# A two-layer graph network on one core: fewer and larger transfers, segment marks picked by matrix products, and a looser tie of gathers to VectorE

## The chip, the cores and the metric

The kernel runs on one core of a Trainium2 chip. The metric is the device time of one execution in microseconds (us). A run gives the time of the whole execution. The profile is of one execution of its own: its span runs from the first to the last recorded instruction, and its execution is a little longer than the span. The engines are PE (TensorE), DVE (VectorE), ACT (ScalarE), POOL (GpSimd) and SP (SyncE, which here only issues transfers). PEld is the weight load that comes before each matmul.

## The reference: what is computed

There are 6250 nodes with 256 features each and 106250 edges, sorted by target; 6250 of the edges lead from a node to itself.

```python
# layer 0: a message per edge, by relation r (0 or 1), summed by target
msgs = where(rel == r, relu(relu(x[src] @ W[r].T + b[r]) @ W[r].T + b[r]), msgs)
agg = segment_sum(msgs, dst)
i, f, g, o = split(agg @ W_ih.T + b_ih + b_hh, 4)
hn = sigmoid(o) * tanh(sigmoid(i) * tanh(g))
x = layernorm(x + mlp3(hn))
# layer 1: attention over the edges and one more self loop per node, 4 heads of 64
h = x @ W
e = leaky_relu(a_src[src] + a_dst[dst], 0.2)
alpha = exp(e - segment_max(e, dst)[dst]) / segment_sum(...)
y = layernorm(segment_sum(h[src] * alpha, dst) + bias + x) * gamma + beta
out = layernorm(x + relu(y))
```

The two expensive things are the reads of a row per edge (x[src] through a table of messages, then h[src]) and the sums by target.

## The kernel before

**Preparation (0 to some 190 us).** The self edges are taken out of the list; 782 tiles of 128 edges are left (`TC`). Seven tiles make a window (`WT`), two windows a group, so there are 112 windows (`NW`) and 56 groups (`NG`). A window's targets lie within 64 slots (`SLOTS`) of nodes; for each edge the kernel stores its slot number in DRAM (`slots`, in bf16, eight tiles to a window). It also stores the marks (`cuts`): for each edge 0 where it has the same target as the edge before it, and a very large negative number where a new target begins. At the same time PE computes both messages of every node into a DRAM table (`parts0`).

**Layer 0 (to some 1175 us).** For every tile GpSimd issues one indirect transfer (`gather`, L1720 in the profile) that fetches 128 rows of 256 numbers by index. The tile is multiplied by a one-hot matrix of slots (L2162), which sums it by target. When a group is done, `turn` and `update` run the gates and the small network for four groups at a time (`quads`; at the end for two groups and then for one). `update` keeps three rows of 256 numbers per node in `keep3`: the layer's output, the output plus the bias, and h. They are stored in DRAM (`kept`, L2107), one group at a time. The rows that layer 1 gathers go to `rows1` (L2097).

**Layer 1 (to the end).** GpSimd gathers a row of 260 numbers per edge (h and the logit) into `G`, a ring of ten windows (70 tiles). The first 21 gathers (`EARLY`) are issued before the last rows of layer 0 are there, and `complete` adds what they lack. Groups are taken in pairs, the last four one by one (`pairs`), 26 pairs and 4 singles in all. For each:

- `ahead` loads the slot numbers (`dB`, L2301, one transfer per window, the window's numbers repeated over 64 partitions) and the marks (`cut`, L2308, one transfer per group, one row per tile and head). It compares the slot numbers with the partition's number (L2315, `ohT`), multiplies by what is known of the targets (L2319) and sums three parts (L2336, `of`).
- `weights` turns the logits (L2359), finds the maximum of each segment by four scans over `cut` (L2366 to L2377), and takes the exponential into `exs` (L2390).
- `weighted` makes a one-hot matrix per group (L1826) and multiplies the gathered rows by their weights (L2405, L2410, L2411, `gw`), a window at a time.
- `sum1` multiplies one or two tiles a step by the one-hot matrix (L2526). At the first tile of a group it loads that group's kept rows (`k3`, L2516).
- `finish` divides, adds the kept rows, normalises twice (L2443 to L2472) and stores the result (L2477). The last group's result is shifted by a product (L2482) and stored at L2491.

**What sets the order.** The schedule is written out by hand: each engine executes its instructions in the order in which the program issues them. The program runs in steps; in layer 1, step t issues the gather of tile t and handles tile t - 4. The parts above are Python generators (chains), and `yield n` lets n steps pass. One generator, `aheads`, goes through all pairs in order: a pair begins at step 14 times its first group (a single group 14 steps earlier than that), or when the pair before it has ended. Buffers come from `ring`, which hands out n tiles of one name in turn. `Pace` ties the gathers to VectorE: at the end of each step it notes VectorE's last instruction, and `hold` lets a gather wait for the note of a given number of steps before it. In layer 1 that distance is 8 steps (`AHEAD1`) and more at the beginning.

```python
move = gather(G[w][:, t - WT * w, :], rows1, idx1[:, t : t + 1])
pace.hold(move, t, AHEAD1 + max(0, 6 * WT - (t - EARLY) // 4))
```

The distance is thus 50 at tile 21 and falls by one in four tiles until it is 8, at tile 189. SyncE issues all the loads and stores named here except the gathers, in the order of the program, so a store that waits for its data holds the loads behind it.

Of the kernel before, what the change touches and what calls it, by code (L numbers as in the profile page):

```python
# [42 lines left out]
P = 128  # L43
N = 6250
D = 256
# [37 lines left out]
BLOCK1, BLOCK2 = 33, 40  # L83
AHEAD_G = range(AHEAD_W // 2)
LATE = 3
AHEAD0 = 2 * WT
AHEAD1 = WT + 1
NOROW = NP + SLOTS - 1
# [656 lines left out]
def gnn_kernel(  # L745
# [47 lines left out]
    slots = dram.tile([NW, (WT + 1) * P], BF16, name="slots")  # L793
    cuts = dram.tile([(NC + 1) * CT, P], F32, name="cuts")
    srcs = dram.tile([EARLY, P], F32, name="srcs")
    kept = dram.tile([NG, P, 3 * D], F32, name="kept")
    packed = dram.tile([2 * BLOCKS, HB], I32, name="packed")

    const = ctx.enter_context(tc.tile_pool(name="fconst", bufs=1))
# [844 lines left out]
def fast(  # L1644
# [57 lines left out]
    def windows_of(g):  # L1702
        return range(2 * g, 2 * g + 2)
# [137 lines left out]
    with (  # L1841
# [134 lines left out]
        def update(groups, aT):  # L1976
# [62 lines left out]
            mv = ring(up, [P, 4, 2], F32, "fmv", 3)  # L2039
            rstd = ring(up, [P, 4], F32, "frstd", 3)  # L2040

            keep3 = [ring(up, [P, 3, D], F32, "keep3", 6) for g in groups]
            for i, g in enumerate(groups):
                u = everyone
                p3 = ring(upp, [P, 4 * P], F32, "fpg", 5)[:, : 2 * P]
# [34 lines left out]
            for i, g in enumerate(groups):  # L2080
                u = everyone
                ph = ring(upp, [P, 4 * P], F32, "fpg", 5)[:, : D + 2 * H]
                for k in range(2):
                    nc.tensor.matmul(  # L2084
                        ph[u, :], hs[i][:, k, u], Wx[:, k, :], start=(k == 0), stop=(k == 1)
                    )
                hr = ring(up, [P, D + 2 * H], F32, "hr", 3)
                if g >= NG - LATE:
                    hr = rows_l[:, g - (NG - LATE), :]
                nc.scalar.copy(hr[u, :], ph[u, :])  # L2090
                nc.scalar.copy(keep3[i][u, 2, :], ph[u, :D])

                in_order(stored, g)
                for w in windows_of(g):
                    if w in at_w:
                        to = rows1[bass.ds(at_w[w], SLOTS), :]
                        keep_row(g, nc.sync.dma_start(to, hr[half_of(w), :HA]))  # L2097
                if g == NG - 1:
                    move = nc.gpsimd.indirect_dma_start(
                        out=rows1,  # L2100
                        out_offset=bass.IndirectOffsetOnAxis(ap=tail_i, axis=0),
                        in_=hr[:, :HA],
                        in_offset=None,
                    )
                    keep_row(g, move)
                yield 1
                nc.sync.dma_start(kept[g, u, :], keep3[i][u, :, :].rearrange("p c f -> p (c f)"))  # L2107

                nd = ring(up, [P, 2, H], F32, "nd", 3)
                left = ring(up, [P, 2, H], F32, "left", 3)  # L2110
                nd3 = ring(up, [P, 3, 2, H], BF16, "nd3", 3)
                nc.vector.tensor_copy(nd[u, 0, :], hr[u, HA : HA + H])  # L2112
                nc.vector.tensor_copy(nd[u, 1, :], hr[u, D:HA])
                lg = loop[u, g, :]
                nc.vector.tensor_add(lg, nd[u, 0, :], nd[u, 1, :])
                n3 = [nd3[u, c, :, :] for c in range(3)]
                nc.vector.tensor_copy(n3[0], nd[u, :, :])
                nc.vector.scalar_tensor_tensor(lg, lg, 0.2, lg, op0=OP.mult, op1=OP.max)
                nc.vector.tensor_sub(left[u, :, :], nd[u, :, :], n3[0])
                nc.vector.tensor_copy(n3[1], left[u, :, :])  # L2120
                nc.vector.tensor_sub(n3[2], left[u, :, :], n3[1])
                yield slow
                for s, w in enumerate(windows_of(g)):
                    nc.scalar.copy(
                        node3[half_of(w), g, s, :, :],
                        nd3[half_of(w), :, :, :].rearrange("p c a h -> p c (a h)"),
                    )

        got, ohs, sums, turned, stored, loop0, rows_x = {}, {}, {}, {}, [], {}, {}
        run.start(weights_of_logits())  # L2130

        def order_of(g):
# [113 lines left out]
    with (  # L2246
# [45 lines left out]
        def ahead(pair, box):  # L2292

            cut = ring(ep, [P, P + 1], F32, "cut", 3)
            of = ring(ep, [P, 2 * GS, 2 * H], F32, "of", 3)
            box.update(cut=cut, of=of)
            dBs = []
            for g in pair:
                dB = ring(ep, [P, W8, P], BF16, "dB", 3)
                for w in windows_of(g):  # L2300
                    nc.sync.dma_start(  # L2301
                        dB[half_of(w), :, :].rearrange("p j e -> p (j e)"),
                        at(slots, w * W8 * P, [[0, SLOTS], [1, W8 * P]]),
                    )
                dBs.append(dB)
            for i, g in enumerate(pair):
                n = len(tiles_in(g)[1])
                nc.sync.dma_start(  # L2308
                    cut[i * GS * H : (i * GS + n) * H, :],
                    at(cuts, tiles_in(g)[0][0] * P, [[P, n], [0, H], [1, P + 1]]),  # L2310
                )
            yield 8
            for i, (g, dB) in enumerate(zip(pair, dBs)):
                ohT = ring(ep, [P, W8, P], BF16, "ohT", 2)
                nc.vector.tensor_scalar(ohT, dB, slot_p, None, op0=OP.is_equal)  # L2315
# [26 lines left out]
                yield 1  # L2342

        def weights(pair, box):
# [10 lines left out]
                return ap.rearrange("p (t h) -> p t h", h=H)  # L2355

            yield 1
            pe = ring(tps, [P, P], F32, "turn", 2)
# [10 lines left out]
            pd = ring(tps, [P, P], F32, "turn", 2)  # L2369
# [11 lines left out]
            pm = ring(tps, [P, P], F32, "turn", 2)  # L2381
# [36 lines left out]
        def finish(g, ps):  # L2418
# [1 line left out]
            u = everyone  # L2420
            n = u.stop
            at_w = lows_of(ws)
            k3 = k3s[g]
# [74 lines left out]
        def sum1():  # L2498
# [12 lines left out]
            if g not in sums:  # L2511
                sums[g] = ring(eps, [P, D + 2 * H], F32, "fps1", 2)
                left[g] = len(tiles_in(g)[1])
                u = everyone
                k3s[g] = ring(fp, [P, 3, D], F32, "k3", 3)
                nc.sync.dma_start(k3s[g][u, :, :].rearrange("p c f -> p (c f)"), kept[g, u, :])  # L2516
            begins = left[g] == len(tiles_in(g)[1])
            left[g] -= 1
            j = t - 2 * WT * g
# [20 lines left out]
        for q in range(2):  # L2540
            nc.vector.tensor_scalar(
                shift[:, q, :], iota_f, own_q[:, q : q + 1], None, op0=OP.is_equal
            )
        run.start(aheads())
        pace = Pace(0)
        t = 0
        while t < TC + LAG or late or queue or run.chains:
            if EARLY <= t < TC:
                w = t // WT
                if t % WT == 0:  # L2550
                    G[w] = ring(rowsp, [P, WT * HA], F32, "G", 10).rearrange(
                        "p (j f) -> p j f", f=HA
                    )
                move = gather(G[w][:, t - WT * w, :], rows1, idx1[:, t : t + 1])
                pace.hold(move, t, AHEAD1 + max(0, 6 * WT - (t - EARLY) // 4))
            k = t - LAG
            if 0 <= k < TC:
                if k < EARLY:
# [91 lines left out]
```

## Time and profile before

| what | us |
|---|---|
| median of 10 runs | 2185.58 |
| lowest and highest run | 2180.65, 2188.49 |
| the profiled execution | 2182.08 |
| its span | 2180.3 |
| PE busy | 1556.4 |
| GpSimd (POOL) busy | 1529.5 |
| VectorE (DVE) busy | 1285.4 |
| ScalarE (ACT) busy | 509.9 |
| first gather of layer 0 starts | 153.7 |
| first ordinary gather of layer 1 starts | 1176.6 |
| last gather starts | 2133.8 |

The page of the profile gives the span in 40 slices of 54.5 us, each digit the busy share of an engine in tenths. A group of instructions is a line, an engine, an operation and its tiles ("G<-rows,fidx" reads `rows` and `fidx` and writes `G`), with its count, its busy time in us, the mean duration of one in ns, and the time for which the engine stood idle just before them, with what ended most of it. "issue" is an idle time for which the profile shows no other reason. In a timeline the columns are the start and the duration in us, the engine, the line, the operation, and in brackets the idle time before. SyncE's transfers are in the trace with the time that SyncE took to issue them: 0.60 us for `dB`, 0.90 us for `cut`, 0.52 us for the store of `kept` and 0.44 us for its load (medians). The gathers of layer 1 bring 128 rows of 1040 bytes each.

### The profile page before, as it was taken

To read this page: it belongs to the slowest core of one execution; us is meant where nothing else is said; L and a number is where in the kernel's file an instruction comes from. 1 tells how busy PE (TensorE), PEld (TensorE's weight loads), DVE (VectorE), ACT (ScalarE), POOL (GpSimd) and SP (SyncE) were. 2 spreads that over 40 slices of the span, in tenths; PEclk is the share of its full clock that TensorE was granted. 3 is DMA by queue.
4 is the path that set the end of the run, shared out by engine and by line. 5 is a ranking of instruction groups with operands and counts; after the bars stand their busy time and mean duration, and the time that the engine had idled before them with its cause. 6 is when DMAs were issued, how large, how long until landed. Compare 5 with 4: busy or idle time off the path is not lost. (4 is left out here: it accounts for less than half of the span.)

```text
span 2180.3 us, 23466 instructions
## 1 busy us (share of the span) xinstructions
PE 1556.4 (71%) x5945; PEld 795.5 (36%) x5945; DVE 1285.4 (59%) x3508; ACT 509.9 (23%) x1571; POOL 1529.5 (70%) x1610
## 2 busy tenths in 40 slices
PE   8996898888888988888996565455554545454564
PEld 5654443333333333333454333232322223232332
DVE  8773244333333334333544788877787777787786
ACT  3332022222212221222343121212111121211212
POOL 2317777777777777777776777777777777777771
PEclk9998899998999989998998776676767666676777
DMA  5337546555545554555556455655556565555551
GB/s 163 127 104 211 170 137 173 144 171 167 153 145 156 172 164 139 147 172 165 171 166 184 126 158 147 165 157 147 156 145 160 146 165 144 159 153 151 158 152 48
DMA packets 164627, 334.53 MB, mean 153 GB/s; under 512 B 42658, under 2 KB 75157, under 8 KB 164482
## 3 DMA queue, kind: packets, MB, share of 16 engines
q0 software_dynamic: 76048, 207.99, 35.6%
q1 hardware_dynamic: 86257, 121.90, 18.0%
q10 hardware_dynamic: 2176, 3.05, 0.5%
q8 instruction: 49, 0.80, 0.2%
q14 instruction: 97, 0.79, 0.1%
HBM read 280.25 MB, written 52.53 MB: 153 GB/s over the span
## 5 line engine op out<-in xcount | busy, mean ns | idle before, releaser
L1720 POOL DMA_INDIRECT G<-rows,fidx x761 | 726.6, 955 | 231.8 <-issue 123.7
L1720 POOL DMA_INDIRECT G<-parts,fidx x722 | 690.6, 956 | 221.6 <-issue 160.1
L2526 PE MATMUL fps<-gw,oh 128*64 128x264 f32 (+1 forms) x1674 | 438.1, 469 | 244.4 <-DVE gw L2411 244.3
L2162 PE MATMUL fps<-G,oh 128*64 128x257 f32 (+1 forms) x1674 | 495.6, 423 | 125.7 <-DMA G<-parts,fidx 101.7
L2526 PEld LDWEIGHTS fps<-gw,oh 128*64 128x64 f32 (+1 forms) x1674 | 224.7, 166 | 412.5 <-DVE gw L2411 263.1
L2162 PEld LDWEIGHTS fps<-G,oh 128*64 128x64 f32 (+1 forms) x1674 | 195.1, 148 | 401.4 <-issue 183.9
L2411 DVE TENSOR_TENSOR gw<-G,bank 128x1792 f32<-128x1792 f32 (+1 forms) x167 | 248.9, 1490 | 62.3 <-ACT gw L2410 58.8
L2001 PE MATMUL fpg<-faT,fWihT 128*128 128x512 f32 (+2 forms) x432 | 170.2, 517 | 0.2 <-DVE faT L1937 0.2
L1919 DVE TENSOR_SCALAR kind<-fps 128x1 f32<-128x1 f32 x112 | 12.4, 152 | 230.7 <-PE fps L2162 230.7
L1826 DVE TENSOR_TENSOR oh<-bank,fslot 128x1024 f32<-128x1024 f32 x106 | 128.8, 1215 | 10.0 <-ACT bank L2390 7.2
L2359 PE MATMUL turn<-fident,e 128*120 128x128 f32 (+2 forms) x30 | 12.4, 415 | 151.5 <-ACT e L2571 151.5
L1609 POOL DMA_INDIRECT G<-parts,fidx x60 | 56.9, 948 | 67.3 <-DMA parts<-fms 49.4
L1575 PE MATMUL fpm<-fWrT,fhT 128*128 128x256 f32 x392 | 94.3, 393 | 8.0 <-DVE fms L1583 6.3
L2001 PEld LDWEIGHTS fpg<-faT,fWihT 128*128 128x128 f32 x432 | 70.6, 189 | 67.4 <-issue 56.8
L2112 DVE COPY nd<-hr 128x4 f32<-128x4 f32 x53 | 10.1, 190 | 142.9 <-ACT hr L2090 142.9
L1561 PE MATMUL fph<-fxc,fWrT 128*128 128x512 f32 (+1 forms) x208 | 90.0, 582 | 5.3 <-DMA frel_i<-in_rel_dram 4.7
L2460 ACT ACTIVATE frs<-fmv,eps_c 128x1 f32<-128x1 f32 x112 | 32.9, 294 | 237.5 <-DVE gw L2405 154.0
L2466 ACT ACTIVATE fy<-fy,frs 128x256 f32<-128x256 f32 x112 | 66.8, 597 | 87.3 <-DVE frs L2463 46.2
L1575 PEld LDWEIGHTS fpm<-fWrT,fhT 128*128 128x128 f32 x392 | 75.3, 196 | 27.7 <-issue 8.9
L2084 PE MATMUL fpg<-Wx,fyT 128*128 128x264 f32 x224 | 76.1, 469 | 3.0 <-ACT fyT L2075 3.0
L2579 ACT COPY e<-G 128x28 f32<-128x28 f32 x112 | 23.8, 213 | 180.1 <-DMA G<-rows,fidx 143.3
L2359 PEld LDWEIGHTS turn<-fident,e 128*120 128x120 f32 (+2 forms) x30 | 4.7, 157 | 165.3 <-ACT e L2571 164.0
(347 smaller groups left out, 1965.6 us busy)
## 6 DMA issues: line engine op xcount, KB each, us to landing
kept<-keep SPq DMA_DIRECT2D x56, 384.0 KB
k<-kept SPq DMA_DIRECT2D x56, 384.0 KB
dB<-slots SPq DMA_DIRECT2D x112, 128.0 KB
loop<-parts SPq DMA_DIRECT2D x110, 128.0 KB
parts<-fms SPq DMA_DIRECT2D x49, 256.0 KB
G<-parts,fidx POOLq DMA_INDIRECT x782
G<-rows,fidx POOLq DMA_INDIRECT x761
fxn<-in_x_dram SPq DMA_DIRECT2D x110, 64.0 KB
```

The lines of the kernel that those rows point to most:

```text
L1561: nc.tensor.matmul(ph[:, :cols], WrT_s[:, r, k, m * P : (m + 1) * P], xc[:, k, :cols], start=(k == 0), stop=(k == 1),)
L1575: made = nc.tensor.matmul(pm[:, r, :], hT[:, r, k, j * P : (j + 1) * P], WrT_s[:, r, k, :], start=(k == 0), stop=(k == 1),)
L1609: nc.gpsimd.indirect_dma_start(out=of[:, n % WT, :D], out_offset=None, in_=parts0[: 2 * P * block, :], in_offset=bass.IndirectOffsetOnAxis ...
L1720: return nc.gpsimd.indirect_dma_start(out=to_tile, out_offset=None, in_=table, in_offset=bass.IndirectOffsetOnAxis(ap=idx, axis=0),)
L1826: nc.vector.tensor_tensor(to[:, :nj, :], iota_s[:, None, :].to_broadcast([P, nj, SLOTS]), of[:, :, None].to_broadcast([P, nj, SLOTS]), op= ...
L2001: nc.tensor.matmul(pg[:, :cols], WihT_s[:, k, c * P : (c + 1) * P], aT[:, k, :cols], start=(k == 0), stop=(k == 1),)
L2084: nc.tensor.matmul(ph[u, :], hs[i][:, k, u], Wx[:, k, :], start=(k == 0), stop=(k == 1))
L2162: nc.tensor.matmul(sums[g][to, :], ohj, got[t], start=begins, stop=ends)
L2411: nc.vector.tensor_mul(gw[:, :, :D].rearrange("p j (h f) -> p j h f", h=H), of[:, :n, :D].rearrange("p j (h f) -> p j h f", h=H), ex[:, o ...
L2460: nc.scalar.activation(r, mv[u, k, 1:2], AF.Ln, bias=eps_c[u])
L2466: nc.scalar.activation(y, y, AF.Identity, bias=m, scale=r)
L2526: nc.tensor.matmul(sums[g][to, :], ohj, gw, start=begins, stop=ends)
```

## The change

There are four edits.

1. **Kept rows.** `kept` is stored and loaded for two groups at once: `keep3` is a ring of three tiles for two groups instead of six for one, `k3` a ring of two tiles for two groups instead of three for one. The store is issued after the second group, the load at the first tile of the first group. The last four groups are still stored and loaded one by one.
2. **Slot numbers.** One transfer brings both windows of a group.
3. **Marks.** The first two pairs load them as before. For all others, the whole list of marks lies in SBUF (`cut_all`, one transfer, started at step 21): seven blocks of 113 rows of 129 numbers. A matmul with a matrix of zeros and ones (`pick`) copies the row of each tile to its four heads in PSUM, and ScalarE copies that to `cut`. The PSUM tiles named "turn", of which there are two, become 129 columns wide and serve this too. The pause in `ahead` after the loads is 12 steps for pairs instead of 8.
4. **Tie.** The distance between gather and VectorE falls by one in six tiles instead of four, so it reaches 8 at tile 273.

```diff
-            keep3 = [ring(up, [P, 3, D], F32, "keep3", 6) for g in groups]
+            for g in groups:
+                if g % 2 == 0:
+                    kept_of[g // 2] = ring(up, [P, 2, 3, D], F32, "keep3", 3)
+            keep3 = [kept_of[g // 2][:, g % 2, :, :] for g in groups]
...
-                nc.sync.dma_start(kept[g, u, :], keep3[i][u, :, :].rearrange("p c f -> p (c f)"))
+                if len(groups) == 1:
+                    nc.sync.dma_start(
+                        kept[g // 2, :, g % 2, :], keep3[i].rearrange("p c f -> p (c f)")
+                    )
+                elif g % 2:
+                    nc.sync.dma_start(
+                        kept[g // 2], kept_of[g // 2].rearrange("p i c f -> p i (c f)")
+                    )
...
-                dB = ring(ep, [P, W8, P], BF16, "dB", 3)
-                for w in windows_of(g):
+                dB = ring(ep, [P, W8 * P], BF16, "dB", 3)
+                nc.sync.dma_start(
+                    dB, at(slots, 2 * g * W8 * P, [[W8 * P, 2], [0, SLOTS], [1, W8 * P]])
+                )
+                dBs.append(dB)
+            if pair in pairs[:2]:
+                for i, g in enumerate(pair):
...
+            else:
+                o = pair[0] % 2 * GS * H
+                n = ((len(pair) - 1) * GS + len(tiles_in(pair[-1])[1])) * H
+                pc = ring(tps, [P, P + 1], F32, "turn", 2)
+                nc.tensor.matmul(
+                    pc[:n, :],
+                    pick[:, pair[0] % 8 // 2, o : o + n],
+                    cut_all[:, pair[0] // 8, :],
+                    start=True,
+                    stop=True,
+                )
+                nc.scalar.copy(cut[:n, :], pc[:n, :])
+            yield 12 if len(pair) > 1 else 8
...
-            yield 8
...
-                k3s[g] = ring(fp, [P, 3, D], F32, "k3", 3)
-                nc.sync.dma_start(k3s[g][u, :, :].rearrange("p c f -> p (c f)"), kept[g, u, :])
+                if g % 2 == 0:
+                    k3s[g // 2] = ring(fp, [P, 2, 3, D], F32, "k3", 2)
+                of = k3s[g // 2].rearrange("p i c f -> p i (c f)")
+                if len(pair_of[g]) == 1:
+                    nc.sync.dma_start(of[:, g % 2, :], kept[g // 2, :, g % 2, :])
+                elif g % 2 == 0:
+                    nc.sync.dma_start(of, kept[g // 2])
...
+        def all_cuts():
+
+            nc.sync.dma_start(
+                cut_all, at(cuts, 0, [[P, CR + 1], [CR * P, -(-TC // CR)], [1, P + 1]])
+            )
+            for q in range(4):
+                nc.vector.tensor_scalar(
+                    row_q[:, q : q + 1], iota_p, float(4 * WT * q), None, op0=OP.subtract
+                )
+                nc.vector.tensor_scalar(
+                    pick[:, q, :].rearrange("p (i t h) -> p i t h", i=2, h=H),
...
+                    row_q[: CR + 1, q : q + 1],
+                    None,
+                    op0=OP.is_equal,
+                )
+                yield 1
+
         run.start(aheads())
+        run.start(all_cuts(), 3 * WT)
...
-                pace.hold(move, t, AHEAD1 + max(0, 6 * WT - (t - EARLY) // 4))
+                pace.hold(move, t, AHEAD1 + max(0, 6 * WT - (t - EARLY) // 6))
```

More of the change, by code (lines that the diff above doesn't have):

```diff
@@ L85 @@
 LATE = 3
+CR = 16 * WT
 AHEAD0 = 2 * WT
@@ L795, in gnn_kernel @@
     srcs = dram.tile([EARLY, P], F32, name="srcs")
-    kept = dram.tile([NG, P, 3 * D], F32, name="kept")
+    kept = dram.tile([NG // 2, P, 2, 3 * D], F32, name="kept")
     packed = dram.tile([2 * BLOCKS, HB], I32, name="packed")
@@ L2129, in fast @@
         got, ohs, sums, turned, stored, loop0, rows_x = {}, {}, {}, {}, [], {}, {}
+        kept_of = {}
         run.start(weights_of_logits())
@@ L2298, in ahead @@
             for g in pair:
-                dB = ring(ep, [P, W8, P], BF16, "dB", 3)
-                for w in windows_of(g):
+                dB = ring(ep, [P, W8 * P], BF16, "dB", 3)
[5 more added lines that the diff above has]
+                for i, g in enumerate(pair):
                     nc.sync.dma_start(
-                        dB[half_of(w), :, :].rearrange("p j e -> p (j e)"),
-                        at(slots, w * W8 * P, [[0, SLOTS], [1, W8 * P]]),
-                    )
-                dBs.append(dB)
+                        cut[i * GS * H : (i + 1) * GS * H, :],
+                        at(cuts, tiles_in(g)[0][0] * P, [[P, GS], [0, H], [1, P + 1]]),
+                    )
+            else:
[11 more added lines that the diff above has]
+            yield 12 if len(pair) > 1 else 8
             for i, g in enumerate(pair):
[L2307 to L2310, printed above, removed]
-                )
-            yield 8
-            for i, (g, dB) in enumerate(zip(pair, dBs)):
-                ohT = ring(ep, [P, W8, P], BF16, "ohT", 2)
-                nc.vector.tensor_scalar(ohT, dB, slot_p, None, op0=OP.is_equal)
+                ohT = ring(ep, [P, W8, P], BF16, "ohT", 2)
+                nc.vector.tensor_scalar(
+                    ohT.rearrange("p j e -> p (j e)"), dBs[i], slot_p, None, op0=OP.is_equal
+                )
                 yield 2
@@ L2357, in weights @@
             yield 1
-            pe = ring(tps, [P, P], F32, "turn", 2)
+            pe = ring(tps, [P, P + 1], F32, "turn", 2)[:, :P]
             nc.tensor.transpose(pe[:rs, :], ef, ident)
@@ L2368, in weights @@
             yield 1
-            pd = ring(tps, [P, P], F32, "turn", 2)
+            pd = ring(tps, [P, P + 1], F32, "turn", 2)[:, :P]
             nc.tensor.matmul(pd[:rs, 0:1], toward[:rs, 0, :rs], b[:, P - 1 : P], start=True, stop=True)
@@ L2380, in weights @@
             yield slow
-            pm = ring(tps, [P, P], F32, "turn", 2)
+            pm = ring(tps, [P, P + 1], F32, "turn", 2)[:, :P]
             nc.tensor.transpose(pm[:, :rs], b, ident[:rs, :rs])
@@ L2422, in finish @@
             at_w = lows_of(ws)
-            k3 = k3s[g]
+            k3 = k3s[g // 2][:, g % 2, :, :]
             sm = ring(fp, [P, 4, H], F32, "sm", 3)
@@ L2543, in fast @@
             )
+        pick = ep.tile([CR + 1, 4, 2 * GS * H], F32, name="pick")
+        row_q = ep.tile([P, 4], F32, name="row_q")
+        cut_all = ep.tile([CR + 1, -(-TC // CR), P + 1], F32, name="cut_all")
+        def all_cuts():
[6 more added lines that the diff above has]
+                )
+                nc.vector.tensor_scalar(
+                    pick[:, q, :].rearrange("p (i t h) -> p i t h", i=2, h=H),
+                    bass.AP(
+                        tensor=iota_f.tensor,
+                        offset=iota_f.offset,
+                        ap=[[iota_f.ap[0][0], CR + 1], [2 * WT, 2], [1, GS], [0, H]],
+                    ),
+                    row_q[: CR + 1, q : q + 1],
[3 more added lines that the diff above has]
+                yield 1
         run.start(aheads())
+        run.start(all_cuts(), 3 * WT)
         pace = Pace(0)
```

## The prediction

> **What bounds the kernel now.** I read the page from the engines' totals to the 40 slices, then the long groups, then GpSimd's timeline, then the tail. The totals name no bound: PE 71%, POOL 70%, DVE 59%. The slices do.
>
> ```profile
> PE   8996898888888988888996565455554545454564
> POOL 2317777777777777777776777777777777777771
> PEclk9998899998999989998998776676767666676777
> ```
>
> POOL stands at 7 from the fourth slice to the last but one, while PE falls from 9 to 5. A constant 7 is an engine that never stops: the groups and the timeline say what the other three tenths are.
>
> ```profile
> L1720 POOL DMA_INDIRECT G<-rows,fidx x761 | 726.6, 955 | 231.8 <-issue 123.7
> L1720 POOL DMA_INDIRECT G<-parts,fidx x722 | 690.6, 956 | 221.6 <-issue 160.1
> ```
> ```profile
> 1162.62 0.94 POOL L1720 DMA_INDIRECT G<-rows,idx_e  x1 [0.30 <-issue]
> ...
> 1171.56 1.00 POOL L2099 DMA_INDIRECT rows<-rows_l,tail_i  x1 [5.34 <-ACT keep L2091]
> ...
> 1176.64 0.95 POOL L1720 DMA_INDIRECT G<-rows,fidx  x1 [0.30 <-issue]
> ```
>
> In each layer a gather costs (726.6 + 231.8) / 761 = 1.26 us: 0.95 of work and a gap of 0.30 that every gather has, whoever is named behind it. From 153.7 us to the end of the last gather at 2134.8 the longer gaps are four of 0.5 to 0.8 us near 235 us and the 5.34 us above, where POOL waits for the last rows of the first layer. So the profiled execution is 153.7 us before the gathers, 1981.1 us of gathers, 45.5 us of tail: a span of 2180.3, with 1.8 us around it 2182.08. The median of the runs shown is 2185.58, 3.5 us more; what I add to the one I add to the other.
>
> **Has the tie (pace.hold) any share in it?** Gather t may not start before VectorE's last instruction of step t - 8 - max(0, 42 - (t - 21)//4). I counted VectorE's instructions of each step in the unrolled program and took their ends from the timeline.
>
> ```profile
> 1392.83 0.15 DVE L2463 SCALAR_TENSOR_TENSOR frs<-fmv,frs 128x1 f32<-128x1 f32 x1
> ...
> 1395.40 0.94 POOL L1720 DMA_INDIRECT G<-rows,fidx  x1 [0.30 <-issue]
> ```
>
> The second line is gather 195, the first is its tie, step 187: met 2.4 us early. That is the least slack up to gather 760. It is 16 us or more for gathers 45 to 100, at least 9.3 up to 150, 6.1 up to 189, 2.4 up to 231, and from there 6.1, typically 11.5, to gather 760; in the last 22 gathers the least is 2.1 us. In layer 0 it is never under 7.3 us. The tie holds nothing in this execution.
>
> **The change, part by part.**
>
> *Merged transfers.* SyncE issues 56 fewer loads of slot numbers, 26 fewer stores and 26 fewer loads of kept rows (30 for 56 each), the bytes stay. By the issue rows (0.60, 0.52 and 0.44 us each) that is 34 + 13 + 11 = 58 us off SyncE. Its worth is 0: the chain that ended last has no SyncE step, and no row shows VectorE waiting for slot numbers or kept rows beyond one 1.9 us at the start of layer 1, where the tie has 31 us. What may come late: the even group's store now waits for the odd group, so its buffer is held longer. The ring is still six groups; the next four groups come 56 gathers = 70 us later. Loads of kept rows for a pair need the pair two before finished, the same distance of three groups as now. A load of 768 KB in one piece can delay gathers behind it. The row for that is the gather's landing, 2.8 to 4.2 us in the chain. The 768 KB at 154 GB/s with the queues 57% busy (270 GB/s when busy) take 2.8 us where 384 KB took 1.4; so 1.4 us later at worst. A gather waits on the one eight before it, 10 us earlier, so POOL doesn't see it.
>
> [...]
>
> *Marks by products.* Out go 52 of 56 loads of 0.90 us on SyncE (47 us, also hidden). In come 24 products for pairs and 4 for single groups: a matmul 113x120 by 129 and a copy on ScalarE. Nearest rows: the transpose L2359, 128*120 128x128, 0.43 us with a weight load of 0.17, and the exp L2390, 128x120, 0.27 us. That is 28 x 0.6 = 17 us on PE and 8 us on ACT. In 1180 to 2130 us PE is busy 519 of 950 and ACT 180, both waiting for VectorE, so I take 0. A cost not shown: ScalarE's copy waits for PE, and queued behind it are the weights' copies (L2410) and normalisations that VectorE waits for. Below it is bounded by 0 (PE stands idle at this point of the step), above by the mean wait of PE for VectorE's gw, 263.1 / 53 = 5.0 us a product. I take the low end: the product comes when the previous pair's queue is almost used up, and VectorE has 35 - 26.7 = 8.3 us free in each 35 us of a pair (1935 to 2040 us), more than 5.0. The set-up is one load of 408 KB and eight small VectorE operations, four of 0.15 and four of 0.31 us (the row of L2541): 1.9 us at steps 21 to 24, where the slack is 16 us: 0.
>
> *Longer yield.* Slot comparison and reductions come four steps later in a pair, still ten steps before they are read. One sequence starts all pairs, so the last pair ends at step 722 instead of 718 and pushes the four single groups back by four steps: the last reductions (L2336, three, 0.60 us at 2125.3) fall on VectorE after 2130.
>
> *The tie.* //6 for //4 leaves gather 195 thirteen steps more, 16 us. A wait that isn't there is not shortened: 0 in this execution. From gather 273 on the two are equal.
>
> **The tail** is where a shift of VectorE's work could show.
>
> ```profile
> 2126.24 0.18 DVE L2459 BATCH_NORM_AGGREGATE fmv<-fst 128x2 f32<-128x6 f32 x1
> ...
> 2130.23 0.16 DVE L2463 SCALAR_TENSOR_TENSOR frs<-fmv,frs 128x1 f32<-128x1 f32 x1 [0.59 <-ACT frs L2461]
> ```
> ```profile
> 2127.47 2.79 DMA G<-rows,fidx
> ...
> 2142.77 5.61 PE fps L2526 x20
> 2148.60 1.92 PE fps L2526 x8
> ...
> 2157.57 7.60 PE fps L2526 x24
> ```
>
> The chain takes its last gather at 2127.47 us, landed at 2130.26; then 50 us run through VectorE, PE and ScalarE with no transfer. The three reductions moved past 2130 add at most 0.6 us. The same end bounds it on the other side: before 2130 that 0.6 was in the chain too, but hidden by the gather. So 0 to 0.6; I take 0.6.
>
> The long gathers are the last term: 112 of 1506 took over 0.98 us and cost 15 us in all, 7 of them in layer 1. There 27 of 66 long ones lie on the slot comparison (59 gathers in all meet it, 5 by chance). [...] The same 56 comparisons stay, moved by four steps, so the term is kept, give or take 3 us (half of the 7).
>
> **Sum:** 2182.1 + 0 + 0 + 0.6 = 2182.7 on the profiled execution's scale, 2186.2 on that of the median: 2186. A measurement of this kernel tells 0.2%, 4.4 us, from no change: 2181.2 to 2189.9 is "same".
>
> **Rivals.**
>
> *The runs without a profile do meet the tie (faster).* They are 3.5 us over the profiled one and the tie is within 2.4 us of holding there. If those 3.5 us are POOL held between gathers 170 and 231, easing returns them, and if the moved comparison misses the gathers by luck 3 us more: 2186 - 6.5 = 2179.5. Against it: the spread of the ten runs (2180.65 to 2188.49) has no two groups.
>
> *ScalarE held by the products (slower).* In the four single groups at the end VectorE has only 70 - 58.6 = 11.4 us free (2065 to 2135 us), 2.85 a group. A hold of 5.0 us each that reaches VectorE costs (5.0 - 2.85) x 4 = 8.6 us: 2195. It decides from a hold of 2.85 us in the last four groups, 8.3 in the pairs before. For it: the tie's slack falls to 2.1 us there, so POOL would be held with VectorE. Against it: ScalarE is 21% busy and PE idle before its weights.
>
> *It does nothing.* The transfers are merged and nobody waited for them; that is my forecast with other words, 2186.
>
> **How the numbers follow.** Forecast 0.58, faster by the eased tie and the long gathers 0.20, slower by ScalarE's hold 0.22. The forecast's own range is 2182 to 2189.5 (3 us of long gathers either way). To leave out no more than 2 in 10 the range goes most of the way to both rivals: 2177 to 2195.
>
> **What would show it.** POOL's gaps: 0.30 us throughout, the 5.3 us at the change of layers, the last gather ending at 2133 to 2137. The tie's slack near gather 195 above 15 us. SyncE's rows halved, the loads of marks down to four and one large. ScalarE's copies of products preceded by under 3 us of wait on PE, mostly under 1. The tail 45 to 47 us. I am wrong if POOL shows new waits (for VectorE: the products; for transfers: the merged loads), if the 5.3 us changes by more than 2, or if gathers take another time than 0.95 us.

## The result

| | before | after |
|---|---|---|
| median, us | 2185.11 (30 runs, 2180.65 to 2188.49) | 2196.96 (9 runs, 2194.71 to 2203.03) |
| ratio, 95% interval | | 1.0057 [1.0049, 1.0065] |
| span of the profiled execution, us | 2180.3 | 2193.6 |
| first gather starts | 153.7 | 152.3 |
| last gather ends | 2134.8 | 2145.8 |
| from there to the end | 45.5 | 47.8 |

The change makes the kernel slower by 11.9 us, 0.57%. The profiled execution stands 13.3 us above that of before, and GpSimd accounts for it: new gaps in layer 1 beyond its ordinary ones +10.6, long gathers +2.6 (nearly all in layer 0, whose gathers took 693.3 us after 690.6), the tail +2.3, less 1.4 at the first gather and 0.7 at the change of layers, together +13.4.

On the page of the changed kernel the 40 slices say little: POOL is at 7 from the fourth slice on as before. The groups give the place: the idle time before the gathers of layer 1 is 242.6 us where it was 231.8, and before those of layer 0 it is unchanged. Beside it stands a new wait, PE's for `ohT`, 85.9 us where it was 3.5.

```profile
POOL 2317777777777777777777677777777777777760
...
L1721 POOL DMA_INDIRECT G<-rows,fidx x761 | 726.7, 955 | 242.6 <-issue 129.8
L1721 POOL DMA_INDIRECT G<-parts,fidx x722 | 693.3, 960 | 221.1 <-issue 159.9
...
L2343 PE MATMUL pn<-node,ohT 128*128 128x48 bf16 x448 | 24.3, 199 | 85.9 <-DVE ohT L2337 85.9
```

GpSimd's timeline shows the two large gaps, one at the start of layer 1 and one near the end; the next longest, 1.30 us, stands at 1507 us. All three have VectorE behind them: these are the tie (`pace.hold`).

```profile
1237.44 0.95 POOL L1721 DMA_INDIRECT G<-rows,fidx  x1 [0.30 <-issue]
1243.73 0.95 POOL L1721 DMA_INDIRECT G<-rows,fidx  x1 [5.33 <-DVE of L2360]
```
```profile
2132.96 0.95 POOL L1721 DMA_INDIRECT G<-rows,fidx  x1 [0.30 <-issue]
2138.12 0.94 POOL L1721 DMA_INDIRECT G<-rows,fidx  x1 [4.22 <-DVE sm L2452]
```

VectorE's timeline just before the first of them, and the view of the tile `dB` (instructions on it, then what their engine waited for), name what VectorE waited for: slot numbers. The last of the three fences is the same view of the kernel before, where no wait for a transfer is listed.

```profile
1217.74 0.48 DVE L2401 TENSOR_TENSOR_SCAN s<-cut,ends,s 120x128 f32<-120x128 f32 x1
1235.67 0.49 DVE L2337 TENSOR_SCALAR ohT<-dB,slot_p 128x1024 bf16<-128x1024 bf16 x1 [17.44 <-DMA dB<-slots]
```
```profile
L2312 SPq DMA_DIRECT2D dB<-slots x56: 534/605/36087, 1174.3 to 2109.7; - x56
...
  DMA dB<-slots: 23.1, 4
```
```profile
L2301 SPq DMA_DIRECT2D dB<-slots x112: 444/596/1209, 1174.1 to 2099.4; - x112
...
  issue: 0.4, 2
```

Four waits, 23.1 us; in before there is none. The first line of the last two fences has minimum, median and maximum of what SyncE needed to issue one load (ns): in the changed kernel one took 36 us, in before the longest took 1.2. SyncE's timeline shows which one, the first behind the load of all marks:

```profile
1175.60 10.44 SPq L2318 DMA_DIRECT2D cut<-cuts  x2
1186.08 0.42 SPq L2579 DMA_DIRECT2D cut_all<-cuts  x1
1186.55 38.72 SPq L2312 DMA_DIRECT2D dB<-slots  x2
1225.32 6.79 SPq L2318 DMA_DIRECT2D cut<-cuts  x2
```

And at the end the chain of work that ended last, which had no SyncE step before, now holds loads of slot numbers of 9 and 10 us:

```profile
2069.26 8.83 DMA dB<-slots
...
2107.18 10.03 DMA dB<-slots
```

The packets in the trace say why. In before the four loads of a pair's slot numbers (64 rows of 2 KB each) had mostly 15 to 18 pieces in flight, and the pair was complete 6.1 us after the first issue (median of 23 pairs). The two merged loads of 128 rows have at most 4 in flight, in two streams: the first half is there after 9.3 us, the whole pair after 16.9. The pieces of the load of all marks come in a single stream, 25 in a us; the first comes only when the merged loads ahead are done, 9.6 us after the issue, and 791 pieces then take 32 us, while SyncE stands at its next issue.

That is **theory N (narrow transfers)**: two transfers are as many bytes as planned, but their pieces come in one or two streams. By the time that the pieces take, the load of all marks keeps 0.8 of the 16 DMA engines busy (25 us of pieces in 32 us) and the merged slot numbers 1.5 (median of 24 pairs). They land late, VectorE waits for them, and the tie passes its lateness to GpSimd. The rival is **theory H**: the products hold TensorE or ScalarE, and VectorE with them (the slower rival of the prediction).

### The profile page after: what moved, and what is told of

It reads as the page before. It is cut to its first block, busy times and chain, and to the rows that moved or that the text cites. A ratio compares the mean times of both kernels' runs of the same rounds, so it can differ in the third digit from the quotient of the medians.

```text
span 2193.6 us, 23332 instructions
## 1 busy us (share of the span) xinstructions
PE 1569.2 (72%) x6001; PEld 799.9 (36%) x6001; DVE 1286.8 (59%) x3516; ACT 513.2 (23%) x1599; POOL 1532.2 (70%) x1610
## 5 line engine op out<-in xcount | busy, mean ns | idle before, releaser
L1721 POOL DMA_INDIRECT G<-rows,fidx x761 | 726.7, 955 | 242.6 <-issue 129.8
L1721 POOL DMA_INDIRECT G<-parts,fidx x722 | 693.3, 960 | 221.1 <-issue 159.9
L2555 PE MATMUL fps<-gw,oh 128*64 128x264 f32 (+1 forms) x1674 | 452.1, 466 | 173.7 <-DVE gw L2435 173.7
L2555 PEld LDWEIGHTS fps<-gw,oh 128*64 128x64 f32 (+1 forms) x1674 | 229.6, 166 | 347.4 <-DVE gw L2435 189.1
L2174 PEld LDWEIGHTS fps<-G,oh 128*64 128x64 f32 (+1 forms) x1674 | 190.1, 145 | 415.5 <-DMA G<-parts,fidx 187.7
L2343 PE MATMUL pn<-node,ohT 128*128 128x48 bf16 x448 | 24.3, 199 | 85.9 <-DVE ohT L2337 85.9
```

The source lines that it names most:

```text
L1721: return nc.gpsimd.indirect_dma_start(out=to_tile, out_offset=None, in_=table, in_offset=bass.IndirectOffsetOnAxis(ap=idx, axis=0),)
L2174: nc.tensor.matmul(sums[g][to, :], ohj, got[t], start=begins, stop=ends)
L2555: nc.tensor.matmul(sums[g][to, :], ohj, gw, start=begins, stop=ends)
```

## The experiments

Ten of the runs (e1 to e4, h1 to h4, i1 and i2) met other chips, three in all, on which the kernel before itself takes 2773 to 2779 us and GpSimd is not back to back; ratios are always to the kernel before on the same chip, and those runs are read for landing times, not for the 12 us. "Lead" is the pause, in steps, between issuing a pair's loads and comparing its slot numbers.

| run | what | ratio to before [95%] | waits of VectorE for slot numbers, us (times) | GpSimd's gaps in layer 1 above 0.33 us, sum of the excess, us |
|---|---|---|---|---|
| after | | 1.0057 [1.0049, 1.0065] | 23.1 (4) | 10.6 |
| f1 | marks over 128 rows | 1.0035 [1.0021, 1.0048] | 7.5 (3) | 7.6 |
| f2 | slot numbers split | 1.0005 [0.9995, 1.0014] | 3.9 (2) | 0.4 |
| f3 | both | 1.0011 [1.0002, 1.0020] | 0.4 (1) | 0.5 |
| f4 | before, slot numbers merged | 1.0395 [1.0380, 1.0410] | 132.5 (47) | 84.8 |
| g1 | after, lead 8 | 1.0229 [1.0206, 1.0253] | 100.3 (46) | 48.2 |
| g2 | both, lead 8 | 1.0012 [1.0003, 1.0021] | none | 0 |
| g3 | after, old tie | 1.0103 [1.0088, 1.0118] | 27.6 (4) | 23.9 |
| g4 | merged across the pair | 1.0013 [1.0004, 1.0023] | 0.5 (1) | 0.8 |

**First set, e1 to e4.** The edits: slot numbers in two transfers (e1), the load of all marks as seven (e2), both (e3), the old tie (e4).

```diff
-                nc.sync.dma_start(
-                    dB, at(slots, 2 * g * W8 * P, [[W8 * P, 2], [0, SLOTS], [1, W8 * P]])
-                )
+                for w in windows_of(g):
+                    nc.sync.dma_start(
+                        dB[half_of(w), :], at(slots, w * W8 * P, [[0, SLOTS], [1, W8 * P]])
+                    )
...
-            nc.sync.dma_start(
-                cut_all, at(cuts, 0, [[P, CR + 1], [CR * P, -(-TC // CR)], [1, P + 1]])
-            )
+            for b in range(-(-TC // CR)):
+                nc.sync.dma_start(
+                    cut_all[:, b, :], at(cuts, b * CR * P, [[P, CR + 1], [1, P + 1]])
+                )
...
-                pace.hold(move, t, AHEAD1 + max(0, 6 * WT - (t - EARLY) // 6))
+                pace.hold(move, t, AHEAD1 + max(0, 6 * WT - (t - EARLY) // 4))
```

> The kernel after, with the slot numbers of a group loaded by two transfers again. Theory N (narrow transfers: the merged load of slot numbers and the load of all marks are each served by one or two of the 16 DMA engines and land late; VectorE waits for them and the tie passes the wait to GpSimd): the load lands in some 3.3 us instead of 9.0, the waits of GpSimd near 2138 us (4.2 us) and the 2.3 us longer tail go, the wait of 5.3 us near 1243 us stays, since the load of all marks still stands before the slot numbers on SyncE: 2197 - 6 = 2191 (2189 to 2193). Rival H (ScalarE held by the copies of the products): nothing changes at the end, 2196 to 2198.

> The kernel after, with the list of all marks loaded by seven transfers of 113 rows instead of one of 7 x 113. Theory N: its 791 pieces no longer pass one engine in 36 us, SyncE is not held at 1186 us, VectorE's wait of 17 us near 1235 us and GpSimd's wait of 5.3 us near 1243 us go: 2197 - 5.5 = 2191.5 (2190 to 2193); the waits at the end stay. Rival H: the start is not due to transfers, 2196 to 2198.

> Both of the above in one kernel: slot numbers by two transfers, marks by seven. Theory N: all of the loss goes, 2183 to 2187, the gaps of GpSimd as in the kernel before. Rival H: the products and their copies are still there, so 2193 or more stays.

> The kernel after with the old tie, which reaches 8 steps at tile 189. Theory N says that the tie is what passes VectorE's late start on to GpSimd: at tile 74 the old tie is five steps tighter, so the wait of 5.3 us near 1243 us grows by 5 x 1.25 = 6 us: 2203 (2201 to 2206). If the tie has no share in the loss: 2196 to 2198.

Ratios of 0.9933 [0.9901, 0.9965], 0.9950 [0.9924, 0.9976], 0.9916 [0.9883, 0.9949] and 0.9944 [0.9913, 0.9975]: here every version is faster than before, and the intervals overlap. POOL stands at 5 to 6 of ten, so an engine that waits costs little; the line is e3's.

```profile
POOL 1243666566566666665545545566565656556561
```

The expected times were worked out for a kernel of 2185 us and were not met; as a verdict on 12 us the set is inconclusive. But the transfers show themselves: with split slot numbers (e1, e3) VectorE never waits over 1.4 us for them, and e2's edit **failed**: seven loads of 113 rows are no faster than one. Six of SyncE's seven issues took 4.1 to 9.4 us, and the pieces still came about every 40 ns. What is slow is not the size of the transfer, so the count 113 was next.

**Both mended, each alone and together (f1, f2, f3).** f2 has e1's edit, f1 reads 128 rows of each block where 113 are used, f3 has both.

```diff
-                    cut_all[:, pair[0] // 8, :],
+                    cut_all[: CR + 1, pair[0] // 8, :],
...
-        cut_all = ep.tile([CR + 1, -(-TC // CR), P + 1], F32, name="cut_all")
+        cut_all = ep.tile([P, -(-TC // CR), P + 1], F32, name="cut_all")
...
-                cut_all, at(cuts, 0, [[P, CR + 1], [CR * P, -(-TC // CR)], [1, P + 1]])
+                cut_all, at(cuts, 0, [[P, P], [CR * P, -(-TC // CR)], [1, P + 1]])
```

> The changed kernel, with the load of all marks over 128 rows of each of the seven blocks in place of 113 (the 15 rows more are never used); its slot numbers stay merged. [...] Rival H (TensorE and ScalarE are held by the products of the marks): no change from the changed kernel, 1.0057, 2197.

> The changed kernel with each group's slot numbers in two transfers again, as in the kernel before; the load of all marks stays as it is. Theory N: slot numbers land 3 to 4 us after issue instead of 9, the gaps of GpSimd after 2126 us (5.7 us together) and the tail's 2.3 us more go, the start may keep its 5.3 us gap, since SyncE is still held behind the load of marks: ratio to the kernel before 1.0025 (1.0005 to 1.0035), about 2190 us where that takes 2185. Rival H: no change from the changed kernel, 1.0057, 2197.

> The changed kernel with both mended: the load of all marks over 128 rows, and slot numbers in two transfers. Theory N: no wait of VectorE for slot numbers over 2 us, no gap of GpSimd over 1 us after the first rows of layer 1, the last gather ends at 2132 to 2137 us: ratio to the kernel before 1.000 (0.998 to 1.002), about 2185 us. Rival H: 1.0057 less nothing, about 2196.

The line of the slot numbers' issues in f1 and in f2 (minimum, median, maximum in ns), and f2's waits:

```profile
L2312 SPq DMA_DIRECT2D dB<-slots x56: 534/604/6217, 1172.9 to 2105.2; - x56
```
```profile
L2313 SPq DMA_DIRECT2D dB<-slots x112: 445/594/30498, 1175.2 to 2101.4; - x112
...
  DMA dB<-slots: 3.9, 2
```

f1: with 15 rows *more* in each block, seven eighths of the pieces are there 4 us after the issue, up to 18 at once; the last eighth follows at 10 to 13 us, behind the merged slot numbers. I had expected all of them within 6. SyncE is held 6.2 us instead of 36. The gap near 1244 us is gone, the gaps at the end stay, 7.6 us in sum; 1.0035 where N had 1.003. f2: SyncE is still held for 30.5 us, yet GpSimd has no gap there, because slot numbers issued late but landed 3.5 us later cost VectorE only 3.9 us. So the start needs both narrow transfers at once, and N was too careful: splitting the slot numbers alone brings the time back, 1.0005 instead of 1.0025. f3 as N had it, but for the last gather, which ends at 2137.8 us. The idle time before the gathers in f3, 232.3 us, is that of before:

```profile
L1721 POOL DMA_INDIRECT G<-rows,fidx x761 | 725.8, 954 | 232.3 <-issue 127.3
```

All the products are in f2 and f3, so H falls. Its own row says the same: in the changed kernel ScalarE's 28 copies of products waited for TensorE once, 1.1 us.

```profile
  PE turn L2326: 1.1, 1
```

**The slot numbers alone, and the lead (f4, g1, g2).** f4 is the kernel before with only the merged load. g1 is the changed kernel with the old pause, g2 the same edit on f3.

```diff
-                for w in windows_of(g):
-                    nc.sync.dma_start(
-                        dB[half_of(w), :, :].rearrange("p j e -> p (j e)"),
-                        at(slots, w * W8 * P, [[0, SLOTS], [1, W8 * P]]),
-                    )
+                nc.sync.dma_start(
+                    dB.rearrange("p j e -> p (j e)"),
+                    at(slots, 2 * g * W8 * P, [[W8 * P, 2], [0, SLOTS], [1, W8 * P]]),
+                )
...
-            yield 12 if len(pair) > 1 else 8
+            yield 8
```

> The kernel before with one part of the change alone: each group's slot numbers in one transfer of 128 rows of 2 KB (marks by DMA, kept rows unmerged, the old tie and the old yield of 8). Theory N: the merged transfer lands about 9 us after issue instead of 3.3; with the yield of 8 it is met sooner than in the changed kernel, so VectorE waits for slot numbers near the end at least, GpSimd shows gaps there: ratio to the kernel before 1.003 (1.001 to 1.008), about 2192 us where that takes 2185. Rival H: the merged slot numbers cost nothing, ratio 0.998 to 1.001.

> The changed kernel with the old lead between the issue of the slot numbers and the passes that read them (yield 8 in place of 12); everything else of the change stays. Theory N: merged slot numbers of a pair land 9 and 17 us after their issue, the old lead is shorter than that, so VectorE waits for them at most pairs (over 60 us in all, as it did with 132 us in the kernel before with merged slot numbers alone), and GpSimd shows gaps of 2 to 5 us at most pairs: ratio to the kernel before 1.030 (1.015 to 1.045), about 2249 us where that takes 2184. The longer lead is then what hides the merged transfers' price. Rival (the merged slot numbers cost nothing, and the 132 us came from the marks by DMA or the old tie beside them): ratio as the changed kernel's, 1.0057.

> The changed kernel with both transfers mended (marks over 128 rows, slot numbers in two transfers) and the old lead of 8. Theory N with the tail put down to the longer lead: slot numbers land 3 us after issue, so a lead of 8 is enough, no gap of GpSimd over 1 us; VectorE's last passes of the one-hot blocks and so the tail come back to before's place, tail 45 to 46 us instead of 47.7: ratio to the kernel before 0.9995 (0.998 to 1.001), about 2183 us. Rival (the tail's 2.2 us come from the products or from the kept rows): tail 47 to 48 us and a ratio of 1.001.

f4 takes 2268.97 us, 85 us more than before: N's direction with more than ten times its size. The reason is the lead. Eight steps of 1.25 us are 10.0 us: in before, VectorE compares the first group 9.6 us after the pair's first load was issued and the second group after 15.7 (medians). In f4 the pair's first half needs 9.7 us and the whole pair 17.6, so VectorE comes too early for both loads of nearly every pair, 47 waits. Twelve steps are 15.0 us: in the changed kernel the two comparisons come after 15.3 and 25.5 us, which the 9.3 and 16.9 us of landing fit into. Two neighbouring waits in f4, of one pair:

```profile
1584.46 0.48 DVE L2314 TENSOR_SCALAR ohT<-dB,slot_p 128x1024 bf16<-128x1024 bf16 x1 [2.66 <-DMA dB<-slots]
1591.98 0.49 DVE L2314 TENSOR_SCALAR ohT<-dB,slot_p 128x1024 bf16<-128x1024 bf16 x1 [2.41 <-DMA dB<-slots]
```

g1 confirms it: without the longer pause the change costs 2.29% instead of 0.57, 2234.33 us, and VectorE waits 46 times. So the longer pause carries about 37 us of the merged loads' price, and it is of no use where they are spread: g2 equals f3. Its tail is 46.8 us, between the two cases I had laid out. The line is g1's.

```profile
  DMA dB<-slots: 100.3, 46
```

**The tie (g3).** e4's edit again.

> The changed kernel with the old tie (one lead step less for every 4 gathers in place of 6). Theory N: the tie passes VectorE's lateness on to GpSimd; a tighter tie passes on more of it, at the start and in the middle of layer 1: ratio to the kernel before 1.008 (1.0055 to 1.015), about 2202 us where that takes 2184, with the gap near 1244 us longer than 5.3 us. Rival (the tie is not met anywhere that matters, as the prediction had it): ratio 1.0057, as the changed kernel.

2208.99 us, by the ratios 0.46% or 10 us over the changed kernel, in N's range. The place was not the one I named: the gap near 1244 us is 5.5 us, nearly as before. Seven new gaps of 0.9 to 2.1 us stand between 1347 and 1412 us, where the old tie has already shrunk and the new one has not; they hold 8.6 us beyond the ordinary 0.30 each. The rest is at the end, where the two ties are equal and f1 has nearly the same gaps.

**Merging is not at fault (g4).** The slot numbers of a pair in two loads again, but each brings one half of the partitions for both groups; marks over 128 rows.

```diff
...
+            dB = ring(ep, [P, 2, W8 * P], BF16, "dB", 2)[:, : len(pair), :]
+            for i in range(2):
+                nc.sync.dma_start(
+                    dB[i * SLOTS : (i + 1) * SLOTS, :, :],
+                    at(
+                        slots,
+                        (2 * pair[0] + i) * W8 * P,
+                        [[0, SLOTS], [2 * W8 * P, len(pair)], [1, W8 * P]],
+                    ),
+                )
...
```

> The changed kernel with marks over 128 rows, and the slot numbers of a pair merged the other way: one transfer for each half of the partitions that holds both groups (64 rows outermost, two pieces of 2 KB in each), so as many transfers and bytes as in the changed kernel, and 64 outermost rows instead of 2. Theory N: it is not the merging but the count of outermost rows that costs; both transfers of a pair land 4 to 5 us after issue instead of 9 and 17, no wait of VectorE for slot numbers over 2 us, no gap of GpSimd over 1 us: ratio to the kernel before 1.0005 (0.999 to 1.002), about 2185 us. Rival (a merged transfer is slow for its bytes, whatever its shape): ratio 1.003 to 1.006 and gaps at the end.

60 loads where the changed kernel has 56, the same bytes: the pair is complete after 5.2 us instead of 16.9, up to 21 pieces at once, 1.0013. The shape decides, not the number of transfers.

**Which counts are narrow (h1, h2, h3).** f1's edit with 116 and 122 rows; and 112 rows and 1 row in two transfers. In the edits a pattern lists step and count of each dimension, the outermost first: the merged slot numbers have 2 there, the load of all marks 113. In all three runs the slot numbers are still merged, so two loads in two streams stand ahead of the marks.

> The changed kernel with the load of all marks over 116 rows of each block in place of 113 (3 rows unused). [...] Rival (only multiples of 16 or 32 are spread): 37 us as with 113. Rival (113 alone is slow for another reason): under 4 us.

> The same over 122 rows. [...] Rival (only multiples of 16 or 32 are spread): 39 us. Rival (rows above 113 are spread alike): under 4 us, as with 128.

> The changed kernel with the 113 rows loaded as 112 and 1, in two transfers. [...] Rival (seven blocks in one transfer are slow, and 128 rows are special): over 15 us.

The longest issue of slot numbers behind the load, in h1, h2 and h3:

```profile
L2312 SPq DMA_DIRECT2D dB<-slots x56: 537/605/13851, 1467.2 to 2664.0; - x56
```
```profile
L2312 SPq DMA_DIRECT2D dB<-slots x56: 4/603/21798, 1483.0 to 2687.5; - x56
```
```profile
L2312 SPq DMA_DIRECT2D dB<-slots x56: 482/604/1382, 1489.4 to 2695.8; - x56
```

Over 112 rows seven eighths of the pieces are there within 4 us and the rest by 13, behind the merged slot numbers, as in f1. Over 122 rows no piece comes before the slot numbers ahead are done, 9.6 us after the issue; then 854 come in about 17 us, 50 in a us, twice the 25 of 113 rows: two streams. Over 116 rows some 400 of the 812 pieces come in the first 10.4 us, beside the two streams of slot numbers, and the other half after them, 50 in a us; the last is there after 18.9 us, with 122 rows after 26.8. So 113 rows come in one stream, 122 in two, and 116 in four by my estimate from the two halves, of which two come after the slot numbers ahead. The longest issue of slot numbers behind the load takes 13.9, 21.8 and 1.4 us where 113 rows made it 36.1, and no rival of the three expectations gave such a time. What makes one count narrow and another not is not shown: the trace does not say which engine moved a piece.

**What is left (h4, i1, i2).** h4 and i1 are one kernel: f2 with the marks of all pairs by DMA, no `cut_all` and no products. i2 is f3 with the kept rows stored and loaded for each group as before.

> The changed kernel with the marks of all pairs by DMA, as in the kernel before (no load of all marks, no products), and slot numbers in two transfers: of the change only the merged kept rows, the lead of 12 and the eased tie are left. If the 2 us of longer tail belong to the products: tail 45 to 46 us and a ratio to the kernel before of 1.000. If they belong to the lead or the kept rows: tail 47 to 48 us, a ratio of 1.001, as with both transfers mended.

> The changed kernel with the marks of all pairs by DMA (no load of all marks, no products) and slot numbers in two transfers: of the change the merged kept rows, the lead of 12 and the eased tie are left. If the 2 us of longer tail belong to the products: tail 45 to 46 us, ratio to the kernel before 1.000 where that takes about 2185. If they belong to the lead or the kept rows: tail 47 to 48 us, ratio 1.001.

> The changed kernel with both narrow transfers mended (marks over 128 rows, slot numbers in two transfers) and the kept rows stored and loaded for each group again. If the merged kept rows hold the 2 us: tail 45 to 46 us, ratio to the kernel before 1.000. If the products or the lead hold them: tail 47 to 48 us, ratio 1.001, as with the kept rows merged.

All three met slow chips, so the question of the 2 us of tail stays open. On the chips where before takes 2185 us, f4 has a tail of 47.4 us without products, merged kept rows, eased tie or longer lead, so none of these is needed for one of that length (though VectorE is late there for its own reason). On the slow chips the ratios are 1.0029 [1.0009, 1.0048], 1.0007 [0.9980, 1.0033] and 0.9920 [0.9891, 0.9949]. i1 and i2 ran on one chip and differ by 0.9%, in the products and in the kept rows; e1 and e3, with products and merged kept rows, have 0.9933 and 0.9916 on another. That points to the products in place of loads of marks as a gain of 0.7 to 1% there, and to none from the merged kept rows, but it is not shown: h4 and e1 ran on different chips, and e3 loads the marks in another way than i2. Why those chips are slower was not tried.

## Why the prediction was wrong

*Merged transfers, "its worth is 0": this is the step that failed.* I counted the issues that SyncE saves and asked who waits for the transfers as they were. I worked out the landing of the merged kept rows by bytes, and that of the slot numbers not at all: I let them land as before. A merged transfer is another transfer. Its landing went from 6.1 to 16.9 us a pair, which by itself costs 85 us (f4), with the longer lead and the eased tie some 5 us (f1 against f3, 2190.55 to 2185.70).

What the landing goes by could be read from the traces: pieces in flight and pieces in a us. The merged slot numbers, with 2 outermost, have at most 4 in flight, where the loads of 64 rows had mostly 15 to 18 (before) and the pair in two halves up to 21 (g4). The marks come in one stream of 25 pieces in a us for 113 rows, two for 122 (50 in a us, h2), by estimate four for 116 (h1), and 18 to 24 pieces at once for 128 (f1, f3, g2, g4).

*"One load of 408 KB … 0": failed too.* By bytes it would take 1.5 us at the 270 GB/s that I had worked out; its pieces take 32 us, and SyncE cannot issue for 36. It costs some 5 us (f1 against the changed kernel: 2190.55 to 2196.96, each on its own chip; 1.0035 to 1.0057), and only together with slow slot numbers (f2).

*Marks by products: right.* The products cost nothing that shows (1.0005 in f2, 1.0011 in f3, both with all products). The rival *ScalarE held by the products* gave 2195, near the 2197 measured, by a mechanism that isn't there.

*Longer yield, 0 to 0.6 us: wrong in kind.* It is worth 37 us in the changed kernel, since it covers the slow landing (g1), and nothing without that (g2).

*The tie, "a wait that isn't there is not shortened": true of before, not of after.* Once VectorE is late, the tie is met, and easing it saves about 0.46% (g3 to after, 1.0103 to 1.0057; 8.6 us of it are the gaps between 1347 and 1412 us). I weighed each part against the old schedule and never against the others. The rival that runs without a profile meet the tie found no support: no mended version came out faster than before on these chips.

*The tail and the long gathers: small.* The tail is +2.3 instead of +0.6, from a cause that stays open. The long gathers of layer 1, the term that I allowed 3 us, cost what they did (6.6 us before, 6.7 after), though 14 of them instead of 27 now lie on the slot comparison, so no run shows that it is what lengthens them; the +2.6 is in layer 0, where I had no term. Three us either way of 2186 also make 2183 to 2189, not 2182 to 2189.5. Of what I named to look for, the layer change (4.6), SyncE's rows and the copies' waits came as said; the gaps, the last gather and the tail did not.

No version beat the kernel before on the chips where it takes 2185 us: f2, f3, g2 and g4 lie at 1.0005 to 1.0013. The intervals of the last three lie just above 1: some 2 us are left, about what the tail grew by.

## What to carry to other kernels

Before you merge two transfers, write down the outermost count of the new pattern: here the slot numbers merged with 2 outermost came in two streams, and a saved issue of 0.6 us was paid with 10 us of landing (16.9 us a pair for 6.1). Merged with 64 rows outermost, the same bytes took 5.2 us (g4). Then compare the new landing with the lead in steps, not the old one. SyncE stood for 36.1 us at the issue behind the narrow load of marks, and the loads behind that one were late as well; and a part that looks idle by itself (a pause, an eased tie) may be the cover of another part, so try each edit alone and without its neighbour.

## What the runs showed of the hardware

- Seven blocks of 516-byte pieces: 113 rows come in one stream, 25 pieces in a us, 32 us (the changed kernel); 128 rows, with more bytes, come in 5 to 7 us where the slot numbers are split (f3, g2).
- Behind the merged slot numbers the last eighth of 128 rows came some 6 us after the others (f1), half of 116 rows came in the first 10.4 us, while the slot numbers still ran (h1), and of 122 rows none before 9.6 us, when they were done (h2).
- SyncE's issue of a load of slot numbers, 0.6 us in the median, took 36.1 us (the changed kernel), 30.5 (f2), 21.8 (h2) and 13.9 (h1) behind the load of all marks.
